# Layer 1's first chunk prepared a step sooner, its sums added ahead of ScalarE's parts, and the third image's last expert products spread out

## The chip, the cores and the metric

The kernel runs on one core of a Trainium2 chip. A core has five engines that each take their own instructions in order: TensorE (PE in the profile; PEld are its weight loads), VectorE (DVE), ScalarE (ACT), GpSimd (POOL) and SyncE (SP), which here issues the DMA transfers. They wait for each other through semaphores. The metric is the device time of one execution in microseconds (us).

## What is computed

The input x has 4 images of 64 channels, 256 by 256, in float32. Two layers follow each other, each added to its input. Cut to what matters:

```python
# layer 0, on g = groupnorm(x)
h = gelu(conv3x3(g, c1_w)); xa, k = split(conv1x1(h, c2_w), 2)
xs = gelu(conv_vertical3(conv_horizontal3(xa)))          # depthwise
w = top2(softmax(mean(xs) @ gate_w.T))                   # per image, 3 experts
out = xs + sum_i w[i] * conv1x1(conv1x1(k, e_w2) * conv1x1(xs, e_w1), e_w3)
x = x + conv1x1(out, proj_w)
# layer 1, on y = groupnorm(x)
h = relu(batchnorm(conv3x3(y, quantized w1)))            # statistics over all images
h = batchnorm(conv3x3(h, quantized w2))
x = x + relu(h + y)
```

The experts' weights depend on the mean over a whole image, so an image's expert products come only when its xs are all made. The batch norms need all four images, so the second convolution starts only when the first is done everywhere.

## The kernel before

**Layout.** The 128 partitions hold 64 channels for each of two rows. An image is 32 octets of rows (NOCT), two octets make a chunk, and there are 16 chunks an image (NCH).

**Layer 0.** For an octet n the functions front_conv_a and front_conv_b make the 3x3 convolution (PSUM tile ps_c) from v_ring, sums and differences of pixels that GpSimd makes in front_v (L484). front_butterfly (m, L550 to L552) and front_h (L558) finish it on ScalarE and VectorE. front_taps_a and front_taps_b make the folded 1x1 and vertical convolution (ps_a), front_taps_h the horizontal one and gelu (t, L607 to L614, and xs, L625). front_proj (ps_p, L656) adds the projection to x and stores it. front_k and front_q (ps_k, ps_q) make the experts' low-rank inputs. divide (L434) is a one-element memset on GpSimd, called tick: it waits for front_taps_a's last matmul, and the first matmuls of the next front_conv_b or front_taps_b wait for it.

**Experts.** gate computes an image's expert weights wm. out_octets makes one octet's expert product (ps_o, L742), adds it to y (L746) and takes statistics (L747); after a chunk's second octet it stores y with four DMAs (L753). out_end turns the statistics into the scale and shift of layer 1's group norm.

**Layer 1's first convolution.** Its input chunk is loaded (conv1_load, yn, L770) and scaled (conv1_affine, L775). Each value is then split into two parts of fewer bits, halves[0] rounded by ScalarE (L346) and halves[1], what rounding left, subtracted by VectorE for the first five row pairs and by GpSimd for the others (both L348). The two cuts of rows are CUTS. The convolution also needs the sums of neighbouring pixels, split likewise: GpSimd adds pixels (s, L356), ScalarE rounds (sum, L362), GpSimd subtracts (sum, L364). conv1_a and conv1_b then make the products of half a chunk (ps_h, 16 matmuls, and ps_hm, 4), ScalarE scales the sum's (m, L327), VectorE combines both (h, L328) and takes statistics (L832). h is stored (L834).

For most chunks the pixels are added right after the affine step (conv1_add), some steps before the halves (conv1_split) and the sums (conv1_sums). For image 0's chunks 0 to 3 conv1_add_sums does the adding and the splitting together, one cut after the other, behind conv1_split.

**Order.** A table, plan, holds calls under keys (step, order within the step), and the calls are made in the order of the keys. From step 124 on the order so made is binding on all five engines. One step is one octet of layer 0; image b starts at step 32 b. CONV1 is step 128. There layer 0's last octets of image 3 end, two steps apart (tail), while layer 1 starts: its products take two steps each. plan_conv1 places layer 1's work of image b from step CONV1 + 65 b, plan_out the experts: image 2's last four octets and image 3's 32 octets lie behind CONV1.

**Buffers.** Tiles come from pools by tag. Tag xs has three buffers and holds both the xs of layer 0 and the pixel sums s. Tag t has one buffer and holds front_taps_h's t. PSUM has two double banks of tag c (ps_c, ps_h), one of tag a (ps_a, ps_hm; the first four ps_hm use c) and one of tag p (ps_p, ps_k, ps_q, ps_o).

Of the kernel before, what the change touches and what calls it, by code (L numbers as in the profile page):

```python
# [18 lines left out]
P = 128  # L19
# [27 lines left out]
GF = GP * W  # L47
NG = NPAIR // GP
# [14 lines left out]
def conv_preact_kernel(ctx: ExitStack, tc: tile.TileContext, io, col128, colset, col64):  # L63
# [30 lines left out]
    def flat(t):  # L94
        return t.rearrange("p a b -> p (a b)")
# [17 lines left out]
    HW = W // 2  # L113
# [27 lines left out]
    work = layers.enter_context(tc.tile_pool(name="work", bufs=2))  # L141
# [14 lines left out]
    def at(step, order, call, *args):  # L156
        plan[step, order].append((call, args))
# [15 lines left out]
    def column(name, n=1):  # L173
        return const.tile([P, n], F32, name=name)
# [3 lines left out]
    end, ends = column("end", 2), column("ends", 2)  # L178
# [158 lines left out]
    CUTS = (0, 5), (5, CPAIR + 1)  # L337

    def split(tiles, y, engines, cuts=CUTS):

        parts = []
        for a, e in cuts:
            upper, lower = (by_pixels(t, a, e) for t in tiles)
            parts.append((upper, lower, y[:, a:e, :].rearrange("p a (j e) -> p a e j", e=2)))
        for upper, _, y in parts:
            nc.scalar.activation(upper, y, AF.Copy)  # L346
        for (upper, lower, y), engine in zip(parts, engines):
            engine.tensor_tensor(lower, y, upper.bitcast(F32), ALU.subtract)  # L348

    def add_pixels(y, name, pool, tag, bufs, size, cuts=CUTS):  # L350

        sums = []
        for a, e in cuts:
            t = pool.tile(size, F32, tag=tag, name=f"s_{name}_{a}", bufs=bufs)
            t = (flat(t) if len(size) > 2 else t)[:, 0 : (e - a) * HW].rearrange("p (a b) -> p a b", b=HW)
            nc.gpsimd.tensor_tensor(t, y[:, a:e, 0::2], y[:, a:e, 1::2], ALU.add)  # L356
            sums.append(t)
        return sums

    def split_sums(tiles, sums, cuts=CUTS):  # L360
        for (a, e), t in zip(cuts, sums):
            nc.scalar.activation(tiles[0][:, a:e, :], t, AF.Copy)  # L362
        for (a, e), t in zip(cuts, sums):
            nc.gpsimd.tensor_tensor(tiles[1][:, a:e, :], t, tiles[0][:, a:e, :].bitcast(F32), ALU.subtract)  # L364

    gn1, gn2, c1s, u12, v_edge, c1_bias = {}, {}, {}, {}, {}, {}
# [397 lines left out]
    y_in, h_out, st_h = {}, {}, {}  # L764
# [16 lines left out]
    def conv1_split(b, k):  # L781

        split(halves[k % 2], y_in[b, k], (nc.vector, nc.vector if b == B - 1 else nc.gpsimd))

    sums_in = {}

    def conv1_add(b, k):
        sums_in[b, k] = add_pixels(y_in[b, k], f"1_{b}_{k}", work, "xs", 3, [P, 2, GF])

    def conv1_add_sums(b, k):  # L790

        y = y_in.pop((b, k))
        for cut in CUTS:
            part = add_pixels(y, f"1_{b}_{k}", work, "xs", 3, [P, 2, GF], (cut,))
            split_sums(sums[k % 2], part, (cut,))

    def conv1_sums(b, k):
        del y_in[b, k]
        split_sums(sums[k % 2], sums_in.pop((b, k)))
# [76 lines left out]
    CONV1 = B * F_STEPS  # L876
# [5 lines left out]
    def plan_front(b):  # L882
        t = b * F_STEPS
        place = tail if b == B - 1 else (lambda step: step)
        for k in range(NCH):
            if b > 0 or k >= 2:
                for call in (front_alloc, front_pad, front_load):
                    at(max(t + 2 * k - 3, 0), 0, call, b, k)
        for n in range(NOCT):
            g = t + n  # L890
            at(g, 1, front_conv_a, b, n, (1, 2))
            at(place(g + 1), 3, front_conv_a, b, n, (0, 3))
            at(place(g + 3), 4, front_taps_a, b, n)
            at(g, 5, divide)
            for step in (g + 1, g + 3):
                if step >= CONV1:
                    at(place(step), 5, divide)
            at(place(g + 4), 6, front_proj, b, n)
            at(g, 7, front_conv_b, b, n, (1, 2))
            at(g, 7.5, front_butterfly, b, n)  # L900
            at(place(g + 1), 8, front_conv_b, b, n, (0, 3))
            at(place(g + 1), 8.5, front_h, b, n)
            if b > 0 or n > 0:
                at(g - 1, 9, front_v, b, n, 1)
            if b > 0 or n > 1:
                at(g - 2, 9.5, front_v, b, n, 0)
            at(place(g + 3), 9, front_taps_b, b, n)
            at(place(g + 3), 11, front_taps_h, b, n)
        for j in range(NG // 4):
            at(place(t + 2 * j + 4), 10, front_k, b, j)  # L910
            at(place(t + 2 * j + 5), 10, front_q, b, j)
        e = place(t + NOCT + 3)
        at_each(((e, 2.5), (e, 5.7), (e, 8.7)) if e < CONV1 else ((e + 1, 12.7), (e + 3, 12.7), (e + 5, 12.7)), gate(b))

    def plan_stats(b, t, per):

        for k in range(NCH):

            before, tags = 3, STATS_IN if b == 1 else STATS_IN[:4]
            at(t + int((k - before) * CG / per), 11.5, stats_load, b, k, *tags[k % len(tags)])  # L920
        for g in range(NG):
            at(t + int(g / per), 3.5, stats_group, b, g)
        e = t + int(NG / per) + 1
        places = (e, 5.4), (e + 1, 5.4), (e + 1, 9.9), (e + 2, 5.4), (e + 2, 9.9), (e + 4, 9.9)
        at_each(places, stats_end(b))

    def plan_out(b, steps, order, end):

        for k in range(NCH):
            for call in (low_load, out_load):  # L930
                at(steps[2 * k - 3] if k > 1 else steps[0] - 2, order + 0.2, call, b, k)
            for i in range(2):
                at(steps[2 * k + i], order, out_octets, b, k, (i,))
        at_each(end, out_end(b))

    conv1_pool, halves, sums = [], [], []
# [13 lines left out]
    def plan_conv1(b):  # L950
        t = CONV1 + b * (NG + 1)
        if b == 0:
            at(t - 4, -1, conv1_first)
            at(t, 12, conv1_open)
        for k in range(NCH):
            load, affine, ready = t + 4 * k - 11, t + 4 * k - 6, t + 4 * k - 4
            if b == 0 and k < 4:

                load, affine, ready = ((t - 4, t - 2, t - 1), (t - 1, t, t + 2), (t + 1, t + 3, t + 4), (t + 5, t + 7, t + 8))[k]
            at(max(load, t + 6) if b == 0 and k > 3 else load, 0, conv1_load, b, k)  # L960
            at(affine, 12.2, conv1_affine, b, k)

            at(ready, 5.5 if (b, k) == (0, 1) else 13.1, conv1_split, b, k)
            if b == 0 and k < 4:
                at(ready, 5.6 if k == 1 else 13.2, conv1_add_sums, b, k)
            else:
                at(affine, 12.3, conv1_add, b, k)
                at(ready, 13.2, conv1_sums, b, k)
        for d in range(NG // 2):
            at(t + 2 * d, 13, conv1_a, b, d)  # L970
            at(t + 2 * d + 1, 13, conv1_b, b, d)
        at(t + NG, 13, conv1_end, b)

    for b in range(B):
        plan_front(b)
        if b < B - 1:
            plan_stats(b + 1, b * F_STEPS + 1, 2.7)
            t = (b + 1) * F_STEPS + 4
            e = t + NOCT + 1
            steps, end = [t + n for n in range(NOCT)], ((e, 5.5), (e + 1, 5.5), (e + 1, 9.95), (e + 2, 5.5))  # L980
            if b == B - 2:

                steps[28:] = (CONV1 + 12 + 2 * n for n in range(4))
                end = [(CONV1 + 20 + i, 12.6) for i in range(4)]
            plan_out(b, steps, 2, end)
        else:
            t, e = CONV1 + 24, CONV1 + b * (NG + 1) - 10
            plan_out(b, [t + (e - 6 - t) * n // (NOCT - 1) for n in range(NOCT)], 12.8, [(e - i, 15) for i in (5, 4, 3, 2)])
        plan_conv1(b)

# [22 lines left out]
    h_in = {}  # L1013
# [17 lines left out]
        split(halves2[i % 2], h_in[i], (nc.vector, nc.vector), cuts)  # L1031

    def conv2_add(i):
        sums_in[i] = add_pixels(h_in[i], f"2_{i}", halves_pool, "s", 2, [P, 5 * HW])

    def conv2_sums(i):
        del h_in[i]
        split_sums(sums2[i % 2], sums_in.pop(i))
# [9 lines left out]
    halves_pool = halves_stack.enter_context(tc.tile_pool(name="halves2", bufs=1, reuse_waits="tile"))  # L1048
# [32 lines left out]
    with tc.manual_schedule(  # L1081
# [15 lines left out]
        for d in range(2 * len(chunks)):  # L1097
            i = d // 2
# [13 lines left out]
    steps = chunks[-KEEP:] + chunks[:-KEEP]  # L1112
# [5 lines left out]
    end = ctx.enter_context(tc.tile_pool(name="end", bufs=2, reuse_waits="tile"))  # L1118
# [15 lines left out]
    for i, (b, k) in enumerate(steps):  # L1134
        if i + AHEAD < len(steps):
            end_load(i + AHEAD)
        y, h = y_of.pop(i), h2.pop((b, k))
# [123 lines left out]
```

## Time and profile before

| | |
|---|---|
| time, median of 3 runs | 3380.22 us (3379.53 to 3382.57) |
| profiled execution | 3380.32 us, its span 3378.5 us |
| PE busy | 2732.3 us, 81% of the span |
| DVE busy | 2701.3 us, 80% |
| ACT busy | 1670.7 us, 49% |
| POOL busy | 1611.0 us, 48% |
| chain that ended last | PE 69%, DMA 12%, DVE 10%, ACT 3%, issue 3% |

The span falls into stages: layer 0 until about 1500 us, layer 1's first convolution until about 2280, its second until about 2875, and an elementwise end. The shares above are means over all of these. On the page, a row of digits gives an engine's busy tenths in 40 slices of 84.5 us each. A timeline row has the start, the length, the engine and line, the tiles written and read, the number of instructions merged, and in brackets the idle time before it and what ended it. A row of the list of waits has who waited for whom, the total in us, how often, and the longest.

### The profile page before, as it was taken

The numbers are of one execution on the slowest core, as the hardware profiler recorded it, in microseconds if no ns is written. First come the engines' busy times: TensorE is split into PE (matmuls) and PEld (weight loads), VectorE is DVE, ScalarE is ACT, GpSimd is POOL, SyncE is SP. The second block draws the span as 40 slices with busy tenths as digits, with TensorE's granted clock in tenths as the row PEclk, the third lists the DMA queues.
The fourth block names the chain that finished last, engine by engine and source line by source line (L and its number), as shares of the span: only waits on it lengthen the run. The fifth ranks groups of instructions, "written<-read, shape, count | busy, mean of one in ns | idle before, by whom it ended". The sixth has DMA issues, their size and how long they took to land.

```text
span 3378.5 us, 60896 instructions
## 1 busy us (share of the span) xinstructions
PE 2732.3 (81%) x24832; PEld 1756.3 (52%) x24832; DVE 2701.3 (80%) x2970; ACT 1670.7 (49%) x1831; POOL 1611.0 (48%) x1833
## 2 busy tenths in 40 slices
PE   2999999999999999996899999998999999300000
PEld 1555545554555545543577776776877878200000
DVE  7676588878888777773899898998999999866666
ACT  0344443343434444343566666767777777422222
POOL 2444544443444444433578777766777777100000
PEclk9999999999999999997899999999999999755555
DMA  8675688878887767773688887664666664599999
GB/s 302 168 186 125 166 261 265 244 210 272 261 252 219 209 187 206 201 216 107 209 301 289 283 293 245 232 252 173 238 238 236 238 231 173 202 412 412 412 412 384
DMA packets 365671, 838.28 MB, mean 248 GB/s; under 512 B 23312, under 2 KB 285968, under 8 KB 302672
## 3 DMA queue, kind: packets, MB, share of 16 engines
q1 hardware_dynamic: 365392, 834.40, 74.9%
q8 instruction: 195, 3.19, 0.4%
q14 instruction: 84, 0.69, 0.1%
HBM read 493.00 MB, written 341.31 MB: 247 GB/s over the span
## 4 chain that ended last, share of the span: by engine, by line
PE 69%; DMA 12%; DVE 10%; ACT 3%; issue 3%; SPq 2%; POOL 2%; ACTq 0%; POOLq 0%; DVEq 0%
PE ps_h L304 24%; PE ps_c L441 19%; DMA y_end<-y_d 10%; PE ps_a L441 9%; PE ps_k L632 3%; PE ps_h2m L304 3%; PE ps_o L742 3%; PE ps_p L441 3%; PE ps_hm L304 2%; PE ps_q L669 2%; DMA yn<-y_d 1%; DVE h L328 1%; DVE st_x L386 1%; DVE half L348 1%; SPq L1148 1%
## 5 line engine op out<-in xcount | busy, mean ns | idle before, releaser
L304 PE MATMUL ps_h<-half,w_q 128*128 128x512 f32 x4096 | 1032.3, 404 | 16.7 <-DVE h L328 10.2
L304 PEld LDWEIGHTS ps_h<-half,w_q 128*128 128x128 f32 x4096 | 777.7, 191 | 248.9 <-issue 30.4
L484 POOL TENSOR_TENSOR v_ring<-x 128x256 f32<-128x256 f32 x1024 | 597.1, 616 | 158.7 <-PE ps_c L441 112.0
L364 POOL TENSOR_TENSOR sum<-s,sum 128x640 fp32r<-128x640 f32 (+1 forms) x256 | 556.1, 2192 | 200.1 <-ACT sum L362 194.4
L328 DVE SCALAR_TENSOR_TENSOR h<-ps_h,scale_w,m 128x1024 f32<-128x1024 f32 x256 | 327.0, 1277 | 101.3 <-ACT m L327 96.7
L441 PE MATMUL ps_c<-v_ring,u 64*64 64x256 f32 (+1 forms) x6472 | 389.2, 371 | 9.6 <-POOL v_ring L484 5.4
L441 PE MATMUL ps_c<-v_ring,c1s 64*64 64x256 f32 (+1 forms) x6472 | 387.7, 369 | 10.8 <-POOL tick L434 10.4
L441 PE MATMUL ps_a<-h,av 64*64 64x512 f32 (+1 forms) x3568 | 383.6, 531 | 3.7 <-DVE t L611 3.6
L441 PEld LDWEIGHTS ps_c<-v_ring,u 64*64 64x64 f32 x6472 | 254.1, 133 | 238.5 <-issue 79.0
L434 POOL MEMSET tick<- 128x1 f32 x132 | 13.1, 99 | 690.5 <-PE ps_a L441 679.7
L441 PEld LDWEIGHTS ps_c<-v_ring,c1s 64*64 64x64 f32 x6472 | 262.6, 133 | 145.4 <-issue 39.6
L550 ACT ACTIVATE m<-ps_c 128x512 f32<-128x512 f32 x128 | 76.6, 599 | 477.3 <-PE ps_c L441 470.3
L625 ACT ACTIVATE xs<-t 128x1024 f32<-128x1024 f32 x128 | 135.3, 1057 | 325.4 <-DVE t L614 292.9
L1139 ACT ACTIVATE v<-y_end,shift,gn 128x2048 f32<-128x2048 f32 x64 | 133.8, 2092 | 320.4 <-DMA y_end<-y_d 313.6
L1140 DVE SCALAR_TENSOR_TENSOR h<-h,ss,v 128x2048 f32<-128x2048 f32 x64 | 150.2, 2351 | 159.6 <-ACT v L1139 159.6
L348 DVE TENSOR_TENSOR half<-h,half 128x1280 fp32r<-128x1280 f32 (+1 forms) x128 | 254.5, 2029 | 7.7 <-ACT half L346 7.7
L608 DVE SCALAR_TENSOR_TENSOR t<-ps_a,m,t 128x1020 f32<-128x1020 f32 x128 | 163.6, 1278 | 110.0 <-ACT t L607 110.0
L656 DVE TENSOR_TENSOR x<-ps_p,x 128x1024 f32<-128x1024 f32 x128 | 156.3, 1221 | 119.0 <-PE ps_p L441 103.6
L441 PEld LDWEIGHTS ps_a<-h,av 64*64 64x64 f32 x3568 | 164.2, 133 | 115.7 <-issue 80.6
L327 ACT ACTIVATE m<-ps_hm,m,scale_w 128x512 f32<-128x512 f32 x128 | 99.5, 778 | 211.2 <-PE ps_hm L304 211.1
L746 DVE SCALAR_TENSOR_TENSOR y<-ps_o,ob,y 128x512 f32<-128x512 f32 x256 | 189.5, 740 | 15.7 <-PE ps_o L742 15.0
L348 DVE TENSOR_TENSOR half<-yn,half 128x1280 fp32r<-128x1280 f32 x80 | 196.7, 2475 | 5.1 <-ACT half L346 5.1
(186 smaller groups left out, 4204.1 us busy)
## 6 DMA issues: line engine op xcount, KB each, us to landing
h_d<-h SPq DMA_DIRECT2D x117, 1024.0 KB, 4.8
h<-h_d SPq DMA_DIRECT2D x64, 1152.0 KB, 7.1
yn<-y_d SPq DMA_DIRECT2D x60, 1152.0 KB, 8.4
xs_in<-in_x SPq DMA_DIRECT2D x64, 1024.0 KB, 8.4
x<-in_x SPq DMA_DIRECT2D x256, 256.0 KB, 5.0
y<-t_d SPq DMA_DIRECT2D x64, 1024.0 KB, 8.6
y_d<-y SPq DMA_DIRECT2D x256, 256.0 KB, 4.5
y_end<-y_d SPq DMA_DIRECT2D x64, 1024.0 KB, 11.3
```

Of the source, the lines that this page charges most:

```text
L304: nc.tensor.matmul(ps[:, 0 : n * HW], w[:, k, m, :], t[:, i + m : i + m + n, c : c + HW], start=(j == 0), stop=(j == len(terms) - 1),)
L328: nc.vector.scalar_tensor_tensor(h.rearrange("p a (b e) -> p e (a b)", e=2), by_two(ps)[:, :, 0 : n * HW], w_scale[w], m.unsqueeze(1).to_b ...
L348: engine.tensor_tensor(lower, y, upper.bitcast(F32), ALU.subtract)
L364: nc.gpsimd.tensor_tensor(tiles[1][:, a:e, :], t, tiles[0][:, a:e, :].bitcast(F32), ALU.subtract)
L441: last[:] = [nc.tensor.matmul(ps[o, at_out[0] : at_out[1], :], w[i], rhs[i], **flags)]
L484: nc.gpsimd.tensor_tensor(v_ring[:, o : o + 2, p, :], *terms[p])
L608: nc.vector.scalar_tensor_tensor(t[:, :, 1:W], ps[:, :, 0 : W - 1], sh[:, 0:1], t[:, :, 1:W], ALU.mult, ALU.add)
L625: nc.scalar.activation(flat(xss[b, n]), flat(t), AF.Gelu, accum_out=pooled[b][:, n : n + 1])
L656: nc.vector.tensor_tensor(t1, ps, t1, ALU.add)
L746: nc.vector.scalar_tensor_tensor(y, ps[:, 2 * n + g], out_bias[b], y, ALU.add, ALU.add)
L1139: nc.scalar.activation(v, y, AF.Identity, bias=shift[:, b : b + 1], scale=gn2[b][:, 1:2])
L1140: nc.vector.scalar_tensor_tensor(h, h, ss2[:, 0:1], v, ALU.mult, ALU.add)
```

## The change

Three things are changed, all in the order of work around step 128.

Image 0's chunk 0 of layer 1 gets its affine step at (125, 5.6) in place of (126, 12.2), and its halves and sums at (126, 5.6) in place of (127, 13.1). Its load stays at step 124.

conv1_prepare takes conv1_add_sums' place for chunks 0 to 3: GpSimd first adds the pixels of both cuts, then the halves are split, then ScalarE rounds both sums and GpSimd subtracts both. The first cut's s lies in the single buffer of tag t, the second's in one of tag xs.

Image 2's last four octets of experts go from steps 140, 142, 144 and 146 to 142, 146, 150 and 154, the four parts of its out_end from steps 148 to 151 to steps 158 to 161, and image 3's 32 octets are spread from step 164 (before: 152) to 307.

In the instructions' order this moves on ACT chunk 0's affine, two halves and two roundings ahead of the octet that they stood behind; on POOL the same chunk's memset, adds, half and subtractions, which now stand between the tick of step 126 and the v_ring of octet 31; on DVE one L348; and on SP the stores and loads of the experts against those of layer 1. The number of instructions is the same on every engine.

```diff
--- before.py
+++ after.py
@@ -347,20 +347,20 @@
         for (upper, lower, y), engine in zip(parts, engines):
             engine.tensor_tensor(lower, y, upper.bitcast(F32), ALU.subtract)
 
-    def add_pixels(y, name, pool, tag, bufs, size, cuts=CUTS):
+    def add_pixels(y, name, places, size):
 
         sums = []
-        for a, e in cuts:
+        for (a, e), (pool, tag, bufs) in zip(CUTS, places):
             t = pool.tile(size, F32, tag=tag, name=f"s_{name}_{a}", bufs=bufs)
             t = (flat(t) if len(size) > 2 else t)[:, 0 : (e - a) * HW].rearrange("p (a b) -> p a b", b=HW)
             nc.gpsimd.tensor_tensor(t, y[:, a:e, 0::2], y[:, a:e, 1::2], ALU.add)
             sums.append(t)
         return sums
 
-    def split_sums(tiles, sums, cuts=CUTS):
-        for (a, e), t in zip(cuts, sums):
+    def split_sums(tiles, sums):
+        for (a, e), t in zip(CUTS, sums):
             nc.scalar.activation(tiles[0][:, a:e, :], t, AF.Copy)
-        for (a, e), t in zip(cuts, sums):
+        for (a, e), t in zip(CUTS, sums):
             nc.gpsimd.tensor_tensor(tiles[1][:, a:e, :], t, tiles[0][:, a:e, :].bitcast(F32), ALU.subtract)
 
     gn1, gn2, c1s, u12, v_edge, c1_bias = {}, {}, {}, {}, {}, {}
@@ -785,14 +785,14 @@
     sums_in = {}
 
     def conv1_add(b, k):
-        sums_in[b, k] = add_pixels(y_in[b, k], f"1_{b}_{k}", work, "xs", 3, [P, 2, GF])
-
-    def conv1_add_sums(b, k):
-
-        y = y_in.pop((b, k))
-        for cut in CUTS:
-            part = add_pixels(y, f"1_{b}_{k}", work, "xs", 3, [P, 2, GF], (cut,))
-            split_sums(sums[k % 2], part, (cut,))
+        sums_in[b, k] = add_pixels(y_in[b, k], f"1_{b}_{k}", [(work, "xs", 3)] * 2, [P, 2, GF])
+
+    def conv1_prepare(b, k):
+
+        places = (work, "t", 1), (work, "xs", 3)
+        sums_in[b, k] = add_pixels(y_in[b, k], f"1_{b}_{k}", places, [P, 2, GF])
+        conv1_split(b, k)
+        conv1_sums(b, k)
 
     def conv1_sums(b, k):
         del y_in[b, k]
@@ -956,15 +956,15 @@
             load, affine, ready = t + 4 * k - 11, t + 4 * k - 6, t + 4 * k - 4
             if b == 0 and k < 4:
 
-                load, affine, ready = ((t - 4, t - 2, t - 1), (t - 1, t, t + 2), (t + 1, t + 3, t + 4), (t + 5, t + 7, t + 8))[k]
+                load, affine, ready = ((t - 4, t - 3, t - 2), (t - 1, t, t + 2), (t + 1, t + 3, t + 4), (t + 5, t + 7, t + 8))[k]
             at(max(load, t + 6) if b == 0 and k > 3 else load, 0, conv1_load, b, k)
-            at(affine, 12.2, conv1_affine, b, k)
-
-            at(ready, 5.5 if (b, k) == (0, 1) else 13.1, conv1_split, b, k)
+            at(affine, 5.6 if affine < t else 12.2, conv1_affine, b, k)
             if b == 0 and k < 4:
-                at(ready, 5.6 if k == 1 else 13.2, conv1_add_sums, b, k)
+
+                at(ready, 5.6 if k < 2 else 13.1, conv1_prepare, b, k)
             else:
                 at(affine, 12.3, conv1_add, b, k)
+                at(ready, 13.1, conv1_split, b, k)
                 at(ready, 13.2, conv1_sums, b, k)
         for d in range(NG // 2):
             at(t + 2 * d, 13, conv1_a, b, d)
@@ -980,11 +980,11 @@
             steps, end = [t + n for n in range(NOCT)], ((e, 5.5), (e + 1, 5.5), (e + 1, 9.95), (e + 2, 5.5))
             if b == B - 2:
 
-                steps[28:] = (CONV1 + 12 + 2 * n for n in range(4))
-                end = [(CONV1 + 20 + i, 12.6) for i in range(4)]
+                steps[28:] = (CONV1 + 14 + 4 * n for n in range(4))
+                end = [(CONV1 + 30 + i, 12.6) for i in range(4)]
             plan_out(b, steps, 2, end)
         else:
-            t, e = CONV1 + 24, CONV1 + b * (NG + 1) - 10
+            t, e = CONV1 + 36, CONV1 + b * (NG + 1) - 10
             plan_out(b, [t + (e - 6 - t) * n // (NOCT - 1) for n in range(NOCT)], 12.8, [(e - i, 15) for i in (5, 4, 3, 2)])
         plan_conv1(b)
 
@@ -1031,7 +1031,7 @@
         split(halves2[i % 2], h_in[i], (nc.vector, nc.vector), cuts)
 
     def conv2_add(i):
-        sums_in[i] = add_pixels(h_in[i], f"2_{i}", halves_pool, "s", 2, [P, 5 * HW])
+        sums_in[i] = add_pixels(h_in[i], f"2_{i}", [(halves_pool, "s", 2)] * 2, [P, 5 * HW])
 
     def conv2_sums(i):
         del h_in[i]
```

## The prediction

> **What bounds the kernel now.** I read the 40 slices first, for where TensorE is not full.
>
> ```profile
> PE   2999999999999999996899999998999999300000
> ...
> PEclk9999999999999999997899999999999999755555
> ```
>
> PE is full but for the first and last slices and for slices 19 and 20 (about 1520 to 1690 us), where its granted clock falls too. That is where layer 0's last octets end and layer 1's first convolution starts, the only stretch that the change touches. The busy times by stretch say how much is open: PE is busy for 67.9 of the 108 us from 1490 to 1598, 68.8 of the 82 to 1680, and then 563.3 of the 580 to 2260. So a microsecond won before 1680 should last to the end.
>
> Next the list of waits from 1500 to 1680, then the chain of waits there (start, length, what):
>
> ```profile
> POOL half L348 <- ACT half L346: 53.7, 8, 17.9
> ...
> ACT sum L362 <- POOL s L356: 29.2, 8, 5.3
> ...
> PE ps_q L669 <- DVE x L656: 19.4, 2, 13.8
> ...
> PE ps_c L441 <- POOL tick L434: 10.4, 1, 10.4
> ```
>
> ```profile
> 1574.14 2.31 ACT half L346 x2
> 1576.52 2.66 POOL half L348
> 1579.19 1.22 POOL s L356
> 1580.43 0.74 ACT sum L362
> 1581.24 1.54 POOL sum L364
> 1582.85 1.05 POOL s L356
> 1584.46 0.77 ACT m L327
> 1585.26 1.29 DVE h L328
> ```
>
> This is the preparation of chunk 2: ScalarE makes its two half parts, GpSimd subtracts one, then adds pixels (s), ScalarE rounds (sum), GpSimd subtracts, adds the second cut, ScalarE rounds again. ScalarE works in order, so m L327 at 1584.46, which PE's banks wait for, stands behind a relay that crosses two engines. Chunks 0, 1 and 3 show the same relay (1516 to 1526, 1541 to 1553, 1597 to 1609). The timelines of POOL and PE give chunk 0's price and one more stall, later:
>
> ```profile
> 1516.43 2.68 POOL L348 TENSOR_TENSOR half<-yn,half 128x1024 fp32r<-128x1024 f32 x1 [11.89 <-ACT half L346]
> ...
> 1525.63 0.26 POOL L434 MEMSET tick<- 128x1 f32 x2
> ```
>
> ```profile
> 1525.94 1.54 PE L441 MATMUL ps_c<-v_ring,c1s 64*64 64x256 f32 x11 [10.40 <-POOL tick L434]
> ...
> 1626.12 1.87 PE L742 MATMUL ps_o<-ranks,wm 32*128 32x512 f32 x4 [4.19 <-DVE y L746]
> 1627.92 6.39 PE L304 MATMUL ps_h<-half,w_q 128*128 128x512 f32 x16
> ```
>
> The tick that lets step 128's matmuls start is queued on POOL behind chunk 0. At 1626 PE waits to run an expert product, because VectorE is late with the previous one after the gate.
>
> **What the skill says.** "TensorE: Matmul & The Clock Gate", Part 1, says that TensorE falls to half clock after an idle window of about 3.4 us and needs about as long a busy one to recover. The trace agrees: after the idle 4.19 us sixteen ps_h take 6.39 us, 4.02 otherwise. "SBUF — State Buffer", section "SBUF: two separate sides", calls the ports that VectorE and GpSimd share an exclusive lock for the whole instruction. The trace agrees: L348 on DVE takes 1.5 us alone and 3.60 at 1599.85, where L348 on POOL began 0.2 us before.
>
> **The change, part by part.** In the plan, step 126 starts on PE at 1485.77, 127 at 1497.62, 128 at 1509.17.
>
> *A, chunk 0 a step sooner.* Moved: on ACT the affine (2.08), two halves (2.40), two roundings (1.37); on DVE one L348 (1.5); on POOL the memset (0.31), two adds (2.29), one half (2.4), two subtractions (2.79). No DMA moves: its load stays in step 124, issued at 1472.2, and the DMA engines were quiet by about 1477. The affine falls in ACT's idle 2.98 us before 1483.21, the memset in POOL's idle 1.36 before 1483.65: both free. In step 126 POOL is free of its tick at 1492.66, DVE of its y at 1492.23, ACT of xs at 1490.62. If DVE takes the port lock first (to 1493.8), POOL's adds end at 1496.1, half at 1498.5, subtractions at 1501.3. Behind them on POOL stands v_ring for octet 31; its first two (0.6 each) are done at 1502.5, and PE wants them at 1497.62: a **new stall of 4.9 us** (3.9 if POOL wins the lock). ACT's m for the butterfly is late by 2 to 3 us and t_27 by 1.8 (its tile t is now also the sum's scratch, read until 1500.0), both inside that stall. In return the tick of step 128 is no longer queued: 10.40 us go. Both stalls cool PE: after the old one c1s, ps_a and ps_k took about 0.9 + 0.9 + 0.6 = 2.4 us more than in the step before; I charge the new one the same. 4.9 + 2.4 - 10.4 - 2.4 = **-5.5**. Ends: -9 (no lock, no cooling), -1 (the stall as long as POOL's whole 8.7 us).
>
> *B, chunk 1.* Both adds come right after the affine (1540.2), so they end while ACT makes the halves; the roundings follow these at once, and t_30, at 1552.54 now, waits only for the first subtraction (1548.8, as it borrows t). That is 3.7 us on ACT; at the first PE wait only 2.04 of it counts (1556.51), but the m and x that follow (1559.93, 1563.25) move on. **-3.5**, ends -2 (DVE's half loses the lock) and -4.8 (POOL's half at 2.4 in place of 4.01).
>
> *C, chunk 2.* The relay from 1576.5 to 1584.46 shrinks to two roundings (1.3 us): m at 1577.8, 6.7 sooner. The adds need t, free when xs_31 is done at 1574.0, just as the halves start. x L656 and PE's ps_q (idle 13.75) follow. DVE's L348 may lose the lock by up to 1.7: **-6**, ends -4.5 and -6.7.
>
> *D, chunk 3.* Same relay, 1599.6 to 1608.6. Its adds can now be made before the halves. What is late next is the gate: its exp needs lg, which DVE has at 1604.6 behind L348. Taking 1605 for m in place of 1610.04: **-5**, ends -2.5 (lock again) and -5.5. PE's idle 4.57 before 1610.86 goes with it.
>
> *E, the third image's experts apart.* ps_o of chunks 14 and 15 go from steps 140, 142, 144, 146 to 142, 146, 150, 154, the norm's end from 148-151 to 158-161. Nothing is added or removed: four times two y and two statistics (2.84 us on DVE, 1.06 on PE), eight y_d writes, a table load of 1.28. Now ps_h(7) starts at 1627.92; it needs L328 of product 5, done at 1622.6, and no longer stands behind an expert product that waits: 5.3 sooner. With DVE free of y in between, products 8 to 10 follow each other at 4.9 (1.06 more with an octet), and product 11 would start at 1646.8 in place of 1658.24: 11.4 sooner. But one octet (1.06) is then still to do, and the stall for the mean of the norm (4.46, and 1.6 of cooling: 3.65 for eight ps_h, 2.0 otherwise) only moves; from L328 to bn_aggr's end is latency, so I keep 5.0 of 6.1. 11.4 - 1.1 - 5.0: **-5.5**, ends -1 and -8. SP: y_d writes (3.46 us of issuing) move behind h_d and yn loads, which they no longer hold up; free, since those lead their use by steps.
>
> *F, the fourth image's experts.* Same 32, now from step 164 to 307 rather than from 152: one in 4.6 steps, not 5. Per octet PE needs 2.3 products of 4.78 + 1.06 = 12.1 us; DVE 2.3 x 2.55 (L328 and two statistics) + 1.15 x 2.59 (L348) + 2.84 = 11.7 (before: 13.0 and 12.4). PE stays the bound, with less slack; the waits for h L328 were 6.6 us in 420. **+1.5**, ends 0 and +8. DMA: 0.81 MB a step for 0.79, on a share of 0.80 to 0.91, stays below full.
>
> Sum: -5.5 - 3.5 - 6 - 5 - 5.5 + 1.5 = -24. The ends add to -34 and -3. The profiled execution took 3380.3 (span 3378.5), the median is 3380.2: **3356**.
>
> **Rivals.** *1. The waits return in another form:* t as scratch ties ACT's t_27 and t_30 to POOL, and the port lock gives back the relay's gain; A -1, B -2, C -4.5, D -2.5, E and F cancel: about 3370. For it: 3.6 us for one L348 in this very stretch; against: the relay's waits for s, 29.2 us on ACT, are removed by order alone. *2. Slower:* F decides. VectorE becomes the bound in steps 164 to 307. Each 0.1 us of DVE above PE's 12.1 per octet costs 3.1 us; break-even with the 25.5 won before is at 12.9, that is with every L348 at 3.6; at 13.2 it is about 3389. Against: L348's mean of 2.59 already has such collisions in it. *3. No change:* the start of layer 1 runs to a floor that the trace does not show (data from memory, say), and PE waits as long for that; 3380. Against: yn's loads are not in the chain there.
>
> **How the numbers follow.** Main forecast 0.78, with 3346 to 3366 of its own; rival 1 0.12, rival 2 0.06, rival 3 0.04. The bounds of A to F and rival 1 make 3341 to 3371. A measurement here tells some 0.2% (6.8 us) from no change: faster 0.90 (main and rival 1), same 0.04, slower 0.06.
>
> **What would show it.** Right: PE's 10.4 us wait for the tick gone and one of 4 to 5 us before ps_c<-v_ring,u in step 127; ACT's wait for s L356 near nothing; ps_q's 13.75 us about half; no 4.19 us before ps_o; PE's waits after 1680 hardly longer. Wrong: a stall in step 127 of over 9 us, t L607 waiting long for sum L364, or PE busy under 95% from the fourth image's first octet to its last.

## The result, and the profile after

The changed kernel took 3368.85 us (median of 4, 3364.82 to 3372.54) beside 3381.39 for the kernel before on the same chip: a ratio of 0.9963, 95% interval 0.9945 to 0.9980. Run once more among later experiments it took 3366.17 (median of 5, 3359.46 to 3371.93; ratio 0.9960, 0.9946 to 0.9973). The median of all nine is 3368.4, which I use below. So the change won 12.5 us the first time and 14.4 the second, some 13. I had forecast 24: the direction was right, the size nearly twice too large, and the value lies outside the main forecast's own 3346 to 3366, though inside the whole range.

The profiled execution took 3364.82, the fastest of its four, so the sum below, made on its trace, shows 15.5 us in the span (3378.5 before, 3363.0 now), a little more than the medians. The slices of the page of after first: PE, then its granted clock.

```profile
PE   2999999999999999997899999998999999300000
...
PEclk9999999999999999998999999999999999655555
```

The two digits that the change was aimed at (slices 19 and 20) went from 6 and 8 to 7 and 8, and the clock's dip from 7 and 8 to 8 and 9. All other digits of PE are as before, so the slices don't tell whether the stretch behind stayed as full. That shows only when one follows a single piece of work through both traces. The end of layer 1's products (where the ps_hm that follow a product's sixteen ps_h start), counted from 0, after against before:

| product | its end, after minus before, us |
|---|---|
| 0, 1 | -10.0, -10.5 |
| 2, 3, 5 | -13.8, -19.2, -24.0 |
| 11, 14 | -34.8, -36.1 |
| 15, 18 | -29.1, -26.8 |
| 28, 32 | -25.1, -21.6 |
| 33, 66, 82 | -20.4, -19.0, -17.3 |
| 98 to the end of the first convolution | -14.5 |

So at product 14 the change led by 36.1 us. Part of this lead was borrowed: the kernel before had by then waited for the norm's mean (4.46 us, and 1.6 at a low clock behind it) and had done two octets of image 3 (2.1 us), which the changed kernel still had before it. The lead then fell by 7 us in one place (product 15) and by 14.6 piece by piece over the next 83 products, some 475 us of time.

The list of waits of after from 1500 to 1680 us (who waited for whom, total, how often, the longest):

```profile
POOL half L348 <- ACT half L346: 29.9, 7, 11.6
...
PE ps_q L669 <- DVE x L656: 12.5, 2, 6.9
...
PE ps_h L304 <- DVE h L328: 5.5, 1, 5.5
ACT t L607 <- POOL sum L364: 5.5, 2, 4.5
...
PE ps_m_y L276 <- DVE mv_y L294: 4.7, 1, 4.7
...
PE ps_c L441 <- POOL v_ring L484: 3.8, 1, 3.8
...
PE ps_o L742 <- DMA ranks<-low_d: 1.6, 1, 1.6
...
ACT sum L362 <- POOL s L356: 0.2, 1, 0.2
```

Against the same list of before: the wait of 10.4 us for the tick is gone, and 3.8 us for v_ring stands in its place. ACT's 29.2 us for the pixel sums are 0.2. The longest ps_q wait went from 13.8 to 6.9. The wait for the norm's mean, ps_m_y, is still there (4.7 us, 4.5 before). The 4.2 us for y behind the gate is gone, but PE now waits 5.5 us for h at the same place, and 1.6 us for ranks is new. New is also that ACT's t waits for a subtraction of the sums (L364), once for 4.5 us: the prediction names this as a sign of being wrong.

ACT's timeline of after shows the relay of chunk 2 gone: from the halves straight to the rounding of both sums, then m.

```profile
1560.57 2.46 ACT L346 ACTIVATE half<-yn 128x1280 fp32r<-128x1280 f32 x2
1562.94 1.24 ACT L362 ACTIVATE sum<-s 128x640 fp32r<-128x640 f32 x2
1564.08 0.75 ACT L327 ACTIVATE m<-ps_hm,m,scale_w 128x512 f32<-128x512 f32 x1
```

From the start of the halves to m are 3.51 us; before it was 10.41 (1574.05 to 1584.46 in ACT's timeline). Now PE's timeline of after, the rows with a wait that matters:

```profile
1501.16 1.96 PE L441 MATMUL ps_c<-v_ring,u 64*64 64x256 f32 x32 [3.77 <-POOL v_ring L484]
...
1568.65 1.94 PE L669 MATMUL ps_q<-xs,m 128*32 128x512 f32 x8 [6.85 <-DVE x L656]
...
1599.51 6.56 PE L304 MATMUL ps_h<-half,w_q 128*128 128x512 f32 x16 [5.48 <-DVE h L328]
...
1650.31 0.58 PE L276 MATMUL ps_m_y<-mv_y,m 128*128 128x1 f32 x2 [4.71 <-DVE mv_y L294]
...
1667.61 1.13 PE L742 MATMUL ps_o<-ranks,wm 32*128 32x512 f32 x4 [1.65 <-DMA ranks<-low_d]
...
1749.76 6.54 PE L304 MATMUL ps_h<-half,w_q 128*128 128x512 f32 x16 [3.38 <-DVE h L328]
...
1930.47 6.61 PE L304 MATMUL ps_h<-half,w_q 128*128 128x512 f32 x16 [3.38 <-DVE h L328]
```

The first five lie in the stretch that the prediction works through. The last two do not: they are at the ends of images 0 and 1 of layer 1, 180 us apart, each an idle of 3.38 us and then sixteen matmuls that take 6.5 and 6.6 us, at a granted clock of 0.57 and 0.56. The kernel before waits 0.88 us at these places, in PE's timeline of before:

```profile
1772.39 5.55 PE L304 MATMUL ps_h<-half,w_q 128*128 128x512 f32 x16 [0.88 <-DVE h L328]
...
1950.46 5.57 PE L304 MATMUL ps_h<-half,w_q 128*128 128x512 f32 x16 [0.88 <-DVE h L328]
```

### The profile page after: what moved, and what is told of

Read it like the earlier page. It is cut to its first block, busy times and chain, and to the rows that moved or that the text cites. A ratio compares the mean times of both kernels' runs of the same rounds, so it can differ in the third digit from the quotient of the medians.

```text
span 3363.0 us, 60903 instructions
## 1 busy us (share of the span) xinstructions
PE 2730.7 (81%) x24832; PEld 1758.7 (52%) x24832; DVE 2707.6 (81%) x2970; ACT 1668.5 (50%) x1831; POOL 1610.5 (48%) x1833
## 4 chain that ended last, share of the span: by engine, by line
PE 71%; DVE 11%; DMA 11%; ACT 2%; SPq 2%; issue 2%; POOL 1%; ACTq 0%; DVEq 0%; POOLq 0%
PE ps_h L304 25%; PE ps_c L441 19%; DMA y_end<-y_d 10%; PE ps_a L441 9%; PE ps_h2m L304 3%; PE ps_k L632 3%; PE ps_o L742 3%; PE ps_p L441 3%; PE ps_hm L304 3%; PE ps_q L669 2%; DVE half L348 2%; DVE h L328 1%; DVE st_x L386 1%; SPq L1148 1%; ACT v L1139 1%
## 5 line engine op out<-in xcount | busy, mean ns | idle before, releaser
L304 PEld LDWEIGHTS ps_h<-half,w_q 128*128 128x128 f32 x4096 | 780.8, 192 | 260.4 <-issue 29.2
L364 POOL TENSOR_TENSOR sum<-s,sum 128x640 fp32r<-128x640 f32 (+1 forms) x256 | 556.6, 2194 | 193.8 <-ACT sum L362 188.2
L328 DVE SCALAR_TENSOR_TENSOR h<-ps_h,scale_w,m 128x1024 f32<-128x1024 f32 x256 | 326.9, 1277 | 92.6 <-ACT m L327 92.4
L348 DVE TENSOR_TENSOR half<-h,half 128x1280 fp32r<-128x1280 f32 (+1 forms) x128 | 254.4, 2029 | 7.7 <-ACT half L346 7.7
L348 DVE TENSOR_TENSOR half<-yn,half 128x1280 fp32r<-128x1280 f32 x80 | 201.9, 2540 | 4.2 <-ACT half L346 4.2
```

Of the source, the lines that this page charges most:

```text
L304: nc.tensor.matmul(ps[:, 0 : n * HW], w[:, k, m, :], t[:, i + m : i + m + n, c : c + HW], start=(j == 0), stop=(j == len(terms) - 1),)
L328: nc.vector.scalar_tensor_tensor(h.rearrange("p a (b e) -> p e (a b)", e=2), by_two(ps)[:, :, 0 : n * HW], w_scale[w], m.unsqueeze(1).to_b ...
```

## The experiments

**My theory after seeing this**: the preparation of the chunks (A to D) is worth what I said; E moved the norm's stall more than it removed it; F costs because of the places that its octets come to. **Rivals**: F costs because there are more octets per us (VectorE's load, rival 2 of the prediction); or A to D are worth little and the time behind product 14 is noise of the clock.

**First round: undo one part.** All four are the changed kernel with one part put back. The nine executions of the changed kernel lie up to 13 us apart, those of the other kernels 2 to 12. So a difference of a few us between two medians (no_a, no_e, phase, v_first and the last two kernels below) is not clear by itself, and the traces have to show what happened.

no_a, chunk 0 as late as before (its sums still both added ahead):

```diff
-  load, affine, ready = ((t - 4, t - 3, t - 2), ...
+  load, affine, ready = ((t - 4, t - 2, t - 1), ...
-  at(affine, 5.6 if affine < t else 12.2, conv1_affine, b, k)
+  at(affine, 12.2, conv1_affine, b, k)
-  at(ready, 5.6 if k < 2 else 13.1, conv1_prepare, b, k)
+  at(ready, 5.6 if k == 1 else 13.1, conv1_prepare, b, k)
```

> The changed kernel with chunk 0 of image 0 back at its old steps (affine at 126, halves and sums at 127), the rest as changed. In the changed kernel's trace the first product stands 10.0 us sooner than before. If what is won before product 14 reaches the end, this kernel takes about 10 us more than the changed one (some 3379 us) and PE's wait for the tick of about 10 us is back. If the later stretch (products 15 to 98) has its own pace and takes up what comes earlier, it takes at most 4 us more.

3370.15 us (ratio 0.9967, 0.9954 to 0.9979): 1.8 above the changed kernel, less than the spread. PE's timeline of no_a shows why so little: with both adds ahead the tick is late by less than before.

```profile
1524.48 1.54 PE L441 MATMUL ps_c<-v_ring,c1s 64*64 64x256 f32 x11 [7.45 <-POOL tick L434]
```

7.45 us and not 10.40, against the 3.77 us that A brings. Part of what I booked under A is thus won by the order of the adds alone.

no_bcd, chunks 1 to 3 prepared in the old order, one cut after the other (chunk 0 as changed):

```diff
-  at(ready, ..., conv1_prepare, b, k)
+  at(ready, ..., conv1_old if k else conv1_prepare, b, k)
```

> The changed kernel with chunks 1 to 3 of image 0 done cut by cut again (half, then add, round and subtract of one cut, then of the other), chunk 0 and the experts as changed. The changed kernel's trace has 14.0 us between the shifts of products 1 and 5 (-10.5 and -24.0). If that reaches the end: 12 to 16 us more than the changed kernel, some 3382 us. If the later stretch takes it up: at most 5 us more.

3378.66 us (0.9993, 0.9985 to 1.0001): 10.3 above. The long ps_q wait is back, in PE's timeline of no_bcd:

```profile
1582.27 1.93 PE L669 MATMUL ps_q<-xs,m 128*32 128x512 f32 x8 [13.77 <-DVE x L656]
```

So the order of adds and parts in chunks 1 to 3 is the largest gain that a single undo shows. The two undos make 12.1 us of the 22.5 that A to D win together (chunks_only, below). Both have E and F in place, and neither undoes the order of chunk 0's adds; how the rest is split stays open.

no_e, the third image's last octets and their norm at their old steps:

```diff
-  steps[28:] = (CONV1 + 14 + 4 * n for n in range(4))
-  end = [(CONV1 + 30 + i, 12.6) for i in range(4)]
+  steps[28:] = (CONV1 + 12 + 2 * n for n in range(4))
+  end = [(CONV1 + 20 + i, 12.6) for i in range(4)]
```

> The changed kernel with image 2's last four expert octets back at steps 140 to 146 and its norm's end at 148 to 151; chunks 0 to 3 as changed, image 3's experts from step 164 as changed. Working of the prediction: E is worth 5.5 us, so 3374 us. Its rival: the wait for the norm's mean, 4.7 us and 2.3 us of cooling in the changed kernel, eats what the spacing won, so within 3 us of the changed kernel.

3369.37 us (0.9971, 0.9959 to 0.9982): no difference that I could tell.

no_f, the fourth image's octets spread from step 152, as before:

```diff
-  t, e = CONV1 + 36, CONV1 + b * (NG + 1) - 10
+  t, e = CONV1 + 24, CONV1 + b * (NG + 1) - 10
```

> The changed kernel with image 3's 32 expert octets from step 152 (one in 5 steps) in place of 164, all else as changed. From product 15 to 98 the changed kernel's lead falls by 12.5 us beside the 2.1 us of two octets not yet done. If the closer spacing or the new places of these octets cause it, this kernel is 6 to 12 us faster than the changed one, some 3358 us, and the idle of 3.4 us before the second product of images 1 and 2 is back at 0.9. If the loss there has another cause, it is within 3 us of the changed kernel.

3361.56 us (0.9947, 0.9935 to 0.9960): 6.8 us **faster** than the changed kernel. F looks like a loss, not the small change that I forecast; chunks_only below puts it clear of the spread. The wait for the mean is even longer here, in PE's timeline of no_f:

```profile
1636.38 1.32 PE L742 MATMUL ps_o<-ranks,wm 32*128 32x512 f32 x4 [3.11 <-DMA ranks<-low_d]
...
1664.04 0.56 PE L276 MATMUL ps_m_y<-mv_y,m 128*128 128x1 f32 x2 [6.35 <-DVE mv_y L294]
```

**Second round: which mechanism?** chunks_only has A to D alone (both edits of no_e and no_f); experts_only, run later, has E and F alone, on the kernel before.

> The changed kernel with both parts on the experts undone (image 2's last octets at 140 to 146, its norm's end at 148 to 151, image 3 from step 152); only chunks 0 to 3 are changed. If the parts add up as the single undos say (experts of image 2: 0.5 us, of image 3: -7.3), this takes some 3362 us. If the spreading of image 2's octets only pays with image 3 at 164, it takes 3366 to 3370. By the prediction's sums (A to D -20): 3360.

> The kernel before with only the experts moved (image 2's last octets at 142 to 154, its norm's end at 158 to 161, image 3 from step 164). If the experts' moves cost what they cost on top of the changed chunks (3368.9 against 3359.4), this is 9 us slower than before, some 3391 us. If their spreading also takes stalls out of the old start of layer 1 (the prediction's 5.5 us), it is within 4 us of before.

chunks_only 3359.36 us (0.9934, 0.9921 to 0.9946): 22.5 us under its kernel before, and 9 better than the whole change. experts_only 3387.06 us (1.0019, 1.0012 to 1.0026): 6.4 us slower than before. E and F together lose whether A to D are there or not. From chunks_only, adding E gives no_f, 2.2 us more (within the spread); adding F gives no_e, 10.0 more (clear of it).

Where does F lose? VectorE's timeline of after, at the end of image 0, the stretch ahead of PE's 3.38 us:

```profile
1742.12 3.63 DVE L348 TENSOR_TENSOR half<-yn,half 128x1280 fp32r<-128x1280 f32 x1
1745.67 0.74 DVE L746 SCALAR_TENSOR_TENSOR y<-ps_o,ob,y 128x512 f32<-128x512 f32 x1
...
1748.43 1.27 DVE L328 SCALAR_TENSOR_TENSOR h<-ps_h,scale_w,m 128x1024 f32<-128x1024 f32 x1
1749.73 1.29 DVE L832 BATCH_NORM_STATS2 st_h<-h 128x6 f32<-128x512 f32 x2
1750.94 0.47 DVE L328 SCALAR_TENSOR_TENSOR h_end<-ps_h_end,scale_w,m_end 128x256 f32<-128x256 f32 x1
```

VectorE takes its work in the order of the plan. The octet of step 191 (two y and two statistics, 1745.67 to 1748.4) was put ahead of image 0's last full product, whose h L328 PE's next image waits for: PE's row at 1749.76 begins as that h ends (1748.43 + 1.27). In VectorE's timeline of before, h comes ahead of the octet:

```profile
1771.05 1.29 DVE L328 SCALAR_TENSOR_TENSOR h<-ps_h,scale_w,m 128x1024 f32<-128x1024 f32 x1 [0.18 <-ACT m L327]
...
1773.58 0.73 DVE L746 SCALAR_TENSOR_TENSOR y<-ps_o,ob,y 128x512 f32<-128x512 f32 x1
```

Before, an octet came every 5 steps and an image of layer 1 is 65 steps long, so it met each image's end in the same phase, one step later. Now 32 octets spread over other steps, one in 4.6, hit steps 191 and 256. phase moves just these two by one step:

```diff
+  steps = [s + 1 if s in (CONV1 + NG - 1, CONV1 + 2 * NG) else s for s in steps]
```

> The changed kernel with two of image 3's 32 expert octets one step later: 191 becomes 192 and 256 becomes 257, so that they stand behind the last full product of images 0 and 1 instead of ahead of it. Nothing else moves, the spacing stays 4.6 steps. If the places at the images' ends cause the loss: PE's two idles of 3.4 us before an image's second product become 0.9, some 7 us less than the changed kernel (3362 us). If VectorE's load per octet (density) causes it: within 2 us of the changed kernel.

3363.83 us (0.9949, 0.9935 to 0.9962): 4.6 us less with two octets of 32 moved by one step each. VectorE's timeline of phase in the same place, then PE's:

```profile
1745.53 3.62 DVE L348 TENSOR_TENSOR half<-yn,half 128x1280 fp32r<-128x1280 f32 x1
1749.33 1.29 DVE L328 SCALAR_TENSOR_TENSOR h<-ps_h,scale_w,m 128x1024 f32<-128x1024 f32 x1 [0.18 <-ACT m L327]
1750.65 1.29 DVE L832 BATCH_NORM_STATS2 st_h<-h 128x6 f32<-128x512 f32 x2
1751.85 0.73 DVE L746 SCALAR_TENSOR_TENSOR y<-ps_o,ob,y 128x512 f32<-128x512 f32 x1
```

```profile
1750.67 4.02 PE L304 MATMUL ps_h<-half,w_q 128*128 128x512 f32 x16 [0.88 <-DVE h L328]
...
1928.64 4.04 PE L304 MATMUL ps_h<-half,w_q 128*128 128x512 f32 x16 [0.88 <-DVE h L328]
```

h now follows the half at once, y comes behind it, and PE waits 0.88 us, as before the change. That it keeps its full clock afterwards is not owed to the place alone: behind the same 0.88 us the kernel before took 5.55 us. By the medians this is about half of F's cost; the difference is within the spread, the waits are not in doubt (3.38 or 3.39 us at both ends in each of the eight traces with octets at steps 191 and 256, 0.63 to 0.88 in the eight others). kept_places tests the rest: density or places? It keeps E and the later start, and as many octets in the stretch as the change has, but puts them at the old steps (162, 167, ...) and makes up the number with two extra ones, at steps 224 and 289.

```diff
+  steps = sorted([*range(t - 2, e - 5, 5), t + 60, t + 125])
```

> The changed kernel, but image 3's 32 octets from step 162 at the places that they had before (every fifth step, 192 and 257 among them), with two more at 224 and 289 in the middle of images, so that as many octets lie in the same stretch as in the changed kernel. If the places cost the 9.5 us: as with image 3 from step 152, some 3361 us. If the number of octets in the stretch costs what moving two of them did not bring back (4.4 us): 3364 to 3367.

3359.58 us (0.9931, 0.9918 to 0.9945), 8.8 under the changed kernel: all of F's loss is gone, with as many octets. PE's timeline of kept_places:

```profile
1747.44 5.40 PE L304 MATMUL ps_h<-half,w_q 128*128 128x512 f32 x16 [0.88 <-DVE h L328]
...
1922.51 4.02 PE L304 MATMUL ps_h<-half,w_q 128*128 128x512 f32 x16 [0.88 <-DVE h L328]
```

The same row of the lists of waits from 1640 to 2130 us, one fence each for after and kept_places:

```profile
PE ps_h L304 <- DVE h L328: 14.2, 8, 3.4
```

```profile
PE ps_h L304 <- DVE h L328: 7.7, 9, 2.6
```

The waits are 8 and 9, and half as long (before: 7.5 in 9). So it is where the octets stand, not how many there are. That VectorE isn't the bound shows in its busy time too: from image 3's first ps_o to its last it is busy for 368.4 of 396.5 us in after (93%), and for 389.1 of 412.6 in the faster chunks_only (94%).

The runs don't show where the whole of the other half went: phase itself still waits 11.5 us for h in this stretch, in 9 waits, the longest 3.3, at other octets.

**E's loss.** In after the four parts of the norm's end stand in steps 158 to 161, one a step. mean_apart sets them two steps apart:

```diff
-  end = [(CONV1 + 30 + i, 12.6) for i in range(4)]
+  end = [(CONV1 + 30 + 2 * i, 12.6) for i in range(4)]
```

> The changed kernel with the four parts of image 2's norm end two steps apart (158, 160, 162, 164) in place of one. If the stall for the mean is only a matter of the mean's matmul standing right behind its statistics, its 4.7 us and about 2.3 us of cooling go: some 3362 us. If VectorE is the late engine there, PE waits for an h instead and the time stays within 2 us of the changed kernel.

3360.99 us (0.9943, 0.9931 to 0.9955): 7.4 less. PE's timeline of mean_apart:

```profile
1655.52 0.38 PE L276 MATMUL ps_m_y<-mv_y,m 128*128 128x1 f32 x2 [1.85 <-DVE mv_y L294]
```

4.71 us became 1.85, and PE kept its clock: the granted clock is 1.00 from 1655.52 to 1659.80, where it was 0.50 from 1650.31 to 1654.40 in after. More than half of the stall that I had carried over as latency was another matter of places.

**A's new stall.** v_first prepares chunk 0 a little later in the same step, at order 9.2, so that GpSimd makes octet 31's v_ring ahead of it; the first sum lies in tag xs, not in t.

```diff
-  places = (work, "t", 1), (work, "xs", 3)
+  places = (work, "t" if k else "xs", 1 if k else 3), (work, "xs", 3)
-  at(ready, 5.6 if k < 2 else 13.1, conv1_prepare, b, k)
+  at(ready, (9.2, 5.6, 13.1, 13.1)[k], conv1_prepare, b, k)
```

> The changed kernel with chunk 0's halves and sums in step 126 behind octet 31's v_ring on GpSimd (order 9.2 in place of 5.6), its first sum in tag xs. The new stall of 3.8 us before ps_c<-v_ring in step 127, and the cooling after it, go; t_27 on ACT comes some 2.6 us later. If A's small worth is due to that stall: 2 to 5 us less than the changed kernel. If t_27's delay takes its place: the same within 2 us.

3364.01 us (0.9948, 0.9936 to 0.9961): 4.4 less. PE's timeline of v_first:

```profile
1498.51 1.96 PE L441 MATMUL ps_c<-v_ring,u 64*64 64x256 f32 x32
1501.57 1.13 PE L742 MATMUL ps_o<-ranks,wm 32*128 32x512 f32 x4 [1.11 <-ACT k L640]
```

The 3.77 us for v_ring are gone; 1.11 us for k come. But product 0 starts at 1522.1 here and at 1522.0 in after, so the traces of these two alone show no gain. All traces together do. Nine kernels have chunk 0 as in the change (after, again, no_bcd, no_e, no_f, chunks_only, phase, kept_places, mean_apart). The stall is 3.8 us in each, and the 32 ps_c behind it take 1.96 us in after alone and 2.87 to 3.69 in the eight others; product 0 starts between 1522.0 and 1527.6, with after the earliest of all. In the four with v_first's order the ps_c take 1.96 us each, and product 0 starts between 1520.4 and 1522.1. What v_first saves is thus mostly the clock that the stall costs in most executions.

**Together.** three_mends has v_first, phase and mean_apart; `again` is the changed kernel itself.

> The changed kernel once more, beside the three others. By its four runs so far 3365 to 3373 us; if the spread comes from the state of the clock in step 127 (a stall of 3.8 us that cools PE in some executions and not in others), its fast runs are those without the slow matmuls of ps_c<-v_ring there.

> The changed kernel with all three mends at once: octet 31's v_ring first, octets at 192 and 257, the norm's parts two steps apart. If the stalls are separate, their gains add: 3368.4 - 4.4 - 4.6 - 7.4 = 3352 us. If they take the place of each other: 3358 to 3361, as the best of them alone.

three_mends 3352.63 us (0.9915, 0.9901 to 0.9928): 15.8 under the changed kernel, clear of the spread, where the medians of the three alone make 4.4 + 4.6 + 7.4 = 16.4. That fits three separate losses, though each of the three numbers is uncertain by some us.

**A better version.** Both have v_first's chunk 0, image 3's octets from step 152 as before with the parts of its out_end two steps apart, and image 2's parts two steps apart. best_old_places leaves image 2's octets where they were; best_two_later has them two steps later:

```diff
-  steps[28:] = (CONV1 + 14 + 4 * n for n in range(4))
-  end = [(CONV1 + 30 + i, 12.6) for i in range(4)]
+  steps[28:] = (CONV1 + 14 + 2 * n for n in range(4))      # best_old_places: + 12
+  end = [(CONV1 + 22 + 2 * i, 12.6) for i in range(4)]     # best_old_places: + 20
-  t, e = CONV1 + 36, CONV1 + b * (NG + 1) - 10
+  t, e = CONV1 + 24, CONV1 + b * (NG + 1) - 10
-  [(e - i, 15) for i in (5, 4, 3, 2)]
+  [(e - i, 15) for i in (5, 3, 1, -1)]
```

> Chunks 0 to 3 as changed, with octet 31's v_ring ahead of chunk 0 on GpSimd; all experts at the places of the kernel before; the parts of both norm ends (images 2 and 3) two steps apart instead of one. From the single runs: 3359.4 (experts at old places), less 4 (v first), less 5 to 8 (means apart): 3348 to 3352 us. If the clock's cooling or VectorE takes the place of the stalls: 3355 to 3359.

> The same, but with image 2's last four octets two steps later each (142, 144, 146, 148) and its norm's end from 150. The wait of 7.9 us for the y of octet 28 behind the gate should fall to the 5.5 us for h: 2 to 4 us less than with the old places. If VectorE is then late with the octets of image 3 that start at 152: no gain, or up to 3 us more.

3349.92 us (0.9909, 0.9895 to 0.9922) and 3346.77 us (0.9902, 0.9888 to 0.9915): the second has the lowest median here, 34 us under before and 21.6 under the change; the 3 us between the two are within the spread. PE's timeline of best_two_later:

```profile
1628.77 0.35 PE L276 MATMUL ps_m_y<-mv_y,m 128*128 128x1 f32 x2 [1.41 <-DVE mv_y L294]
1633.09 2.08 PE L742 MATMUL ps_o<-ranks,wm 32*128 32x512 f32 x4 [3.97 <-DMA ranks<-low_d]
...
1745.41 4.02 PE L304 MATMUL ps_h<-half,w_q 128*128 128x512 f32 x16 [0.88 <-DVE h L328]
```

The wait for the mean is 1.41 us, the image's end 0.88. What is left is 3.97 us for ranks, a load that the prediction leaves out.

## Why the prediction was wrong on the experts and right on the chunks

Two steps of the prediction failed, F (+1.5 by mean loads) and E (the norm's stall "only moves", 5.0 us of it): together they were forecast at -4.0 us and measured at +9.0 on top of A to D (the nine executions of the change against chunks_only), +6.4 without A to D (experts_only). A to D were forecast at -20 and measured at -22.5.

- **A, forecast -5.5: right, as far as the traces tell.** The tick's 10.40 us went and 3.77 us for v_ring came (forecast 3.9 to 4.9). In the nine traces with this chunk 0, product 0 starts 4.4 to 10.0 us sooner than before, 5.5 in the middle; the 10.0 of after is the luckiest, since there alone the stall cost no clock. In no_a, where only the order of chunk 0's adds is left, product 0 starts 1.7 sooner, so a part of the 5.5 belongs to that order. Undoing A costs 1.8 us in the times, within the spread: what A alone is worth to the end stays open. v_first shows that the new stall was avoidable.
- **B, C, D, forecast -14.5: the mechanism right, the size within its ends.** From product 1 to product 5 the trace wins 13.5, and undoing them costs 10.3 us. The three are not separated.
- **E, forecast -5.5: failed, in the terms for the stall, "I keep 5.0 of 6.1", and for the octet outstanding.** The front came as worked out: between the traces of chunks_only and no_f, which differ by E alone, product 11 starts 11.5 us sooner (forecast 11.4). But product 16 starts 2.4 us later: no_f waits 6.35 us for the mean and 3.11 for ranks, so it gave back 13.9 us where I had counted 6.1. In after the mean took 7.0 us at product 15, 4.71 idle and the rest at a low clock. In the times E is worth nothing: 2.2 us lost at F's old places (no_f against chunks_only), 0.2 at kept_places, both within the spread. I took "from L328 to bn_aggr's end is latency" as a property of the work; mean_apart takes away more than half of the wait by order alone.
- **F, forecast +1.5: failed, and this is the main miss.** Measured: +10.0 alone on chunks_only, +6.8 on top of E. I divided loads: 12.1 us per octet for PE, 11.7 for VectorE, so PE stays the bound. Busy times in after are 12.3 and 11.9 per octet, near what I had worked out (L348 was longer than my 2.59 us: 2.88 in the mean before and 3.00 after, in the stretch of these octets). PE did stay the bound, and yet it lost, since the sum was a mean and the loss lies at single places. An octet is 2.84 us that VectorE does in one go; standing just ahead of an h that PE waits for, it costs nearly that (3.38 us in place of 0.88), and the clock on top. My range for F, up to +8, came near the size, for a reason (rival 2, VectorE as the bound) that kept_places rules out with as many octets.
- **Rival 1** (3370) gave nearly the measured number by luck, by waits that came back elsewhere than it said: its terms for A to D, -10 in all, are refuted by chunks_only. **Rival 3** is refuted by the same run.
- **The signs that I had named as right**: the tick, the wait for s and ps_q came as written, the v_ring stall a little shorter. The 4.19 us before ps_o went, but 5.48 for h came just behind the gate. The one that failed was "PE's waits after 1680 hardly longer": they doubled (14.2 us for h in place of 7.5). **Of the signs of being wrong** one came: t L607 waited 4.5 us for sum L364, but it does so in chunks_only too, so it is not what the experts' moves lost. PE's busy share from image 3's first ps_o to its last did not fall under 95%: it was 96.5% (382.5 of 396.5 us) with cooled matmuls counted as busy, where before it was 97.9% and in chunks_only 98.4%. That sign was too coarse to see F's loss.
- **The range**: the ends -34 and -3 on 3380 make 3346 to 3377; the stated 3341 to 3371 does not follow from them.

Still open: how the half of F's loss that phase does not give back is split over the shorter waits (1.5 to 3.3 us each) and the clock, and A alone.

## What to carry to other kernels

When work is spread anew over an in-order engine, mean loads alone prove little: look at each place where another engine waits for the one that takes the work, and at what now stands ahead of it there. An old spacing may fit a period of the kernel (here 5 into 65) without saying so. And before a stall is carried over as latency, ask which of its pieces only wait their turn.

## What the runs showed of the hardware

TensorE lost its clock after short idles as well. At the end of image 0 PE was idle for 0.34 to 0.37 us before the two small ps_hm_end and for 0.88 after them, in before, phase, kept_places and three_mends alike. The sixteen ps_h that follow took 4.02 us in phase (granted clock 1.00), 5.40 in kept_places (0.71), 5.55 in before (0.69) and 6.77 in three_mends (0.55). The prediction charged cooling only to idles of 4 us and more, and these idles are far shorter than the window of 3.4 us that it names, yet the clock fell behind them in three of the four. Why the same idles end so differently is not shown. The same stall of 3.8 us in step 127, too, was followed by full speed in the profiled execution of after (32 ps_c in 1.96 us) and by slower matmuls in the eight other traces that have it. From PE's timelines of again and of phase:

```profile
1500.59 3.15 PE L441 MATMUL ps_c<-v_ring,u 64*64 64x256 f32 x32 [3.78 <-POOL v_ring L484]
```

```profile
1501.68 3.69 PE L441 MATMUL ps_c<-v_ring,u 64*64 64x256 f32 x32 [3.77 <-POOL v_ring L484]
```

This makes the start of product 0 vary, by 5.6 us among these nine traces and by 1.7 among the four without the stall. Whether it also makes the whole times vary is not shown: executions of kernels with the stall lie 4.4 us (kept_places) to 13 us (the change) apart, of kernels without it 2.4 (best_old_places) to 9.8 (v_first).
